# Expert layers in fp32 on TensorE: a third split block product in the first layer, a new order of its passes, and sums on GpSimd

## Chip, cores and metric

The kernel runs on one core of one Trainium2 chip. The metric is the device time of one execution in microseconds (us). Three runs of the kernel before took 2548.86, 2551.64 and 2551.95 us, median 2551.64. Differences below about 0.2% can't be told from none.

## What is computed

`x` is 4096 tokens of 512 values, `ctx` 3202 rows of 512. A gated cross attention comes first, then a gated mixture of experts; both add onto `x`. Only the second half matters here:

```
gates = softmax(layernorm(x) @ w_router + b_router)        # 8 experts
topv, topi = top_k(gates, 2)                               # 2 experts a token
buf[e, slot] = the tokens of expert e                      # 640 slots an expert
h   = gelu(buf[e] @ w1[e] + b1[e])                         # 512 -> 2048
out = h @ w2[e] + b2[e]                                    # 2048 -> 512
y   = gate-weighted sum of a token's two rows of out
x   = x + tanh(g_ffn) * y
```

All of it is in fp32, and the kernel does the experts' matrix products by block schemes with seven products instead of eight (Strassen's, in the form of Winograd): sums of blocks are formed on VectorE ahead, and the products' results are added onto each other in PSUM.

## The kernel before

The attention half, the router and the scatter of the tokens into slots fill the first 1590 us of the trace, and the change doesn't touch them. Then comes a loop over the eight experts (L2428), some 120 us each, in which TensorE's instructions stand in an order written out by hand. So do those of VectorE, ScalarE (ACT) and the load queue: the helpers `dv`, `ac`, `ld` and `mm` (L2019 to L2029) chain every instruction behind the one before it on its engine. GpSimd's gathers and stores are not chained.

**The first layer.** The tokens of an expert lie transposed in `bT` (640 columns, two halves of 320, `HC`), the weights in two halves of four feature blocks. An outer split into seven products, numbered 0 to 6, gives four results per feature block: `lo` and `hi`, each for both halves of the columns. `hidden(e, idx)` (L2257) is one pass, and there are eight, for idx 0 to 7. `product(ps, k)` (L2274) is one of the seven: two matmuls of 320 columns. It may accumulate onto a region that ACT has first filled with another region's content (`nc.scalar.copy(Y, X)`, L2302; `copy(Z, Y)`, L2311). A pass takes six PSUM banks: X in bank 0, Q in 1, Y in 2 or 3 in turn, Z in 4, W in 5. Product 0 goes into X, 4 onto a copy of X in Y, 5 onto a copy of Y in Z, 3 into Q, 1 onto X. VectorE then adds Q (copied to SBUF as `p5`, L2306) onto Y and Z (L2319, L2329) into `hT`, and ACT applies the gelu. Gelus that can't go at once are put into the list `owed`, and `due(n)` (L2282) lets ACT do some of them later.

**The split parts.** For the first six feature blocks, three pairs, products 2 and 6 are not done like that. Each is itself split into seven for a pair of feature blocks: seven matmuls of 160 columns. `parts` (L2217) makes them in three steps, which are laid between the products of another pass: one part in each of the passes 1 to 6 (product 6 of a pair in an odd pass, product 2 in the even pass behind it). A part takes a tile of the transposes' pool `ps_tr` (regions X, W, Q) and a bank for its regions Y and Z. Its steps need sums of weight blocks (`deep_w`, L2204: four VectorE instructions of 128 columns) and of token blocks (`deep_x`, L2193: four of 160 columns, once per expert). At the end four VectorE adds (L2247 to L2250) put its results onto `hT`, and two gelus are owed.

**The order of a pass** is product 0, step one, product 3, step two, product 4, step three, product 1, product 5 (L2297 to L2320), with the ACT copies between. In expert 0 the first four feature blocks have products 0 and 1 done ahead (`early`), and their passes go another way (L2286).

**Around the passes**, the main loop lays further VectorE work: sums of weights for this expert's second half (`w1_sums`), sums for the second layer (`left`, `right`), the bias (L2474, L2476). The second layer is a sequence of plain products and five `deep` groups (R7, R6, R5, R4, R3 in the order of the code; L2396), whose left and right sums are kept in two sets of seven tiles, `sets[0]` and `sets[1]`. `sets[0]` is last read by R4, `u2` by the adds of L2571. The rows that an expert has summed up are stored by five indirect DMAs on GpSimd's queue (`send`, L2510); the next expert's five gathers (L2438) wait until those have landed, and the bias adds wait for the gathers.

Of the kernel before, what the change touches and what calls it, by code (L numbers as in the profile page):

```python
# [8 lines left out]
AF = mybir.ActivationFunctionType  # L9
# [5 lines left out]
P = 128  # L15
# [5 lines left out]
def gated_layer(ctx, tc, x, x_t, ctxt, ctxt_t, ctxt_c, ctxt_r, g_xattn, g_ffn, w_sim, w_sim_r, b_sim, W_qv, W_qv_t, b_qv, b_qv_c, w_router, b_router, w1, b1, w2, b2, out):  # L21
# [1976 lines left out]
    with ExitStack() as s3:  # L1998
# [176 lines left out]
        def rows_of(ti, s):  # L2175
# [9 lines left out]
            k: (b, [flat_set[i][:, q * HH : (q + 1) * HH] for q in range(3)] + [p7[:, i - 5, :HH]])  # L2185
            for k, i, b in (("2", 5, xT[2]), ("6", 6, B22))
        }

        def w_of(k, pair):
            n = 3 * (2 * (pair % 2) + (k == "6"))  # L2190
            return [flat_set[2 + (n + q) // 4][:, (n + q) % 4 * P : ((n + q) % 4 + 1) * P] for q in range(3)]

        def deep_x(k):  # L2193

            b, (t1, t2, t4, t3) = x_of[k]
            b11, b12, b21, b22 = (b[:, c, d : d + HH] for c in range(2) for d in (0, HH))
            return [
                lambda: tt(t1, b12, b11, ALU.subtract),
                lambda: tt(t2, b22, t1, ALU.subtract),
                lambda: tt(t3, b22, b12, ALU.subtract),  # L2200
                lambda: tt(t4, b21, t2, ALU.subtract),
            ]

        def deep_w(e, k, pair):  # L2204
# [12 lines left out]
        def parts(e, k, pair, c_bank):  # L2217

            XWQ = ps_tr.tile([P, DC, P], F32, name=f"d{e}_{k}{pair}", tag="tr").rearrange("p c t -> p (c t)")
            X, W, Q = (XWQ[:, i * HH : (i + 1) * HH] for i in range(3))  # L2220
            YZ = banks[c_bank][:, : 2 * HH]
            Y, Z = YZ[:, :HH], YZ[:, HH:]
            a = w1_forms(e, pair // 2)[int(k)]
            f = pair % 2 * 2 * P
            a11, a12, s3, a22 = (a[:, c, f + r : f + r + P] for r in (0, P) for c in range(2))
            s1, s2, s4 = w_of(k, pair)
            b, (t1, t2, t4, t3) = x_of[k]
            b11, _, b21, b22 = (b[:, c, d : d + HH] for c in range(2) for d in (0, HH))
            dst = hT[:, 0, 2 * pair : 2 * pair + 2, HC:] if k == "6" else hT[:, 1, 2 * pair : 2 * pair + 2, :HC]

            def first():
                mm(X, a11, b11, True, True)
                mm(Q, s1, t1, False, True)
                mm(W, a22, t4, False, True)
                ac(lambda: nc.scalar.copy(Y, X))  # L2235

            def second():
                mm(Y, s2, t2, False, True)
                ac(lambda: nc.scalar.copy(Z, Y))
                mm(X, a12, b21, False, True)  # L2240

            def third():
                mm(Z, s3, t3, False, True)
                mm(Y, s4, b22, False, True)

            adds = [
                lambda: tt(dst[:, :, HH:], dst[:, :, HH:], Q.unsqueeze(1).to_broadcast([P, 2, HH]), ALU.add),  # L2247
                lambda: tt(dst[:, :, :HH], dst[:, :, :HH], XWQ[:, : 2 * HH].rearrange("p (f t) -> p f t", f=2), ALU.add),
                lambda: tt(dst[:, 0, HH:], dst[:, 0, HH:], Y, ALU.add),
                lambda: tt(  # L2250
                    dst[:, 1, :].rearrange("p (d t) -> p d t", d=2), dst[:, 1, :].rearrange("p (d t) -> p d t", d=2),
                    Z.unsqueeze(1).to_broadcast([P, 2, HH]), ALU.add,
                ),
            ]
            return first, second, third, adds, dst

        def hidden(e, idx):  # L2257

            h, f = divmod(idx, KQ)
            col = e * NF + h * KH + f  # L2260
            lo, hi = hT[:, 0, idx, :], hT[:, 1, idx, :]
            bias_of = lambda i, n: (lambda c: b1_t[:, c : c + 1])(e * NF + i // KQ * KH + i % KQ + n * KQ)
            b_lo, b_hi = bias_of(idx, 0), bias_of(idx, 1)
            A = [[a[:, k, f * P : (f + 1) * P] for k in range(2)] for a in w1_forms(e, h)]
            X, Q, Y, Z, W = (banks[i][:, :HC] for i in (0, 1, 2 + idx % 2, 4, 5))
            p5 = p5s[idx % 2]
            there = e == 0 and f in early and h == 0
            split = idx < DEEP_IDX
            part = None
            if 1 <= idx <= DEEP_IDX:  # L2270
                k, pair = ("6", idx // 2) if idx % 2 else ("2", idx // 2 - 1)
                part = parts(e, k, pair, 5 if split else 2 + (idx + 1) % 2)

            def product(ps, k, start=False):  # L2274
                for i in range(2):
                    mm(ps, A[k][i], XS[{2: 6, 6: 2}.get(k, k)][i], start and i == 0, i == 1)

            def step(i):
                if part:
                    part[i]()  # L2280

            def due(n):  # L2282
                ac(*owed[:n])
                del owed[:n]

            if there and idx:  # L2286
                ac(lambda: nc.scalar.copy(Y, early.pop(f)))  # L2287
                step(0)
                product(Y, 4)
                due(1)  # L2290
                ac(lambda: nc.scalar.copy(Z, Y))
                step(1)
                product(Q, 3, True)
                ac(lambda: nc.scalar.copy(p5, Q))
                step(2)
                due(1)
            else:  # L2297
                if there:
                    ac(lambda: nc.scalar.copy(Y, early.pop(f)))
                else:  # L2300
                    product(X, 0, True)
                    ac(lambda: nc.scalar.copy(Y, X))  # L2302
# [8 lines left out]
                ac(lambda: nc.scalar.copy(Z, Y))  # L2311
                step(2)
                due(1)
            if not there:
                product(X, 1)
                ac(lambda: nc.scalar.activation(lo[:, :HC], X, AF.Gelu, bias=b_lo))
            due(len(owed))
            if split:
                dv(lambda: tt(lo[:, HC:], Y, p5, ALU.add))  # L2319
            product(Z, 5)  # L2320
            if part:
                dv(*part[3])
                n = int(k == "2")
                for i in range(2):
                    owed.append(
                        lambda d=part[4][:, i, :], b=bias_of(2 * pair + i, n): nc.scalar.activation(d, d, AF.Gelu, bias=b)
                    )
            ac(lambda: nc.scalar.copy(hi[:, :HC] if split else W, Z))
# [99 lines left out]
        for e in range(E):  # L2428
# [4 lines left out]
            ld(lambda: nc.sync.dma_start(b2_t, b2[e].partition_broadcast(P)))  # L2433
            if e == 0:
                dv(*deep_w(0, "6", 0), *deep_x("6"), *coefs(0))
            cf, ti = cf_of[e], ti_of[e]
            for s in range(NST):
                gather = nc.gpsimd.indirect_dma_start(  # L2438
                    out=accs[s][:, :], out_offset=None,
                    in_=out[:, :], in_offset=rows_of(ti, s), bounds_check=N - 1, oob_is_err=False,  # L2440
                )
# [14 lines left out]
            for idx in range(2 * KQ):  # L2456
# [8 lines left out]
                    dv(*deep_w(e, "2", 0), *deep_x("2"))  # L2465
                if idx in (1, 3):
                    dv(*deep_w(e, "6", 1 + idx // 2), *deep_w(e, "2", 1 + idx // 2))
                if idx in (4, 6, 7):
                    k = (0, 2, 4)[(4, 6, 7).index(idx)]
                    dv(left(1, k, k + 2), left(3, k, k + 2))  # L2470
# [175 lines left out]
```

## Time and profile before

| what | value |
|---|---|
| median of three runs | 2551.64 us |
| profiled execution: its own time | 2551.32 us |
| its span, first to last instruction | 2549.5 us |
| granted TensorE clock, mean | 0.999 |
| TensorE matmul busy | 2533.4 us, 14258 instructions |
| VectorE busy | 1976.1 us |
| ACT busy | 715.4 us |
| GpSimd busy | 274.5 us |

A matmul in fp32 is two weight loads and two MATMULs in the trace. In a group's name, `bank` is one of the six PSUM banks, `d` a part's tile, `l` a tile of the two sets. A bracket behind an instruction says how long its engine had been idle before it, and whose end released it. Rows of the view in order of time merge instructions of one kind that follow each other (x4).

### The profile page before, as it was taken

The numbers are of one execution on the slowest core, as the hardware profiler recorded it, in microseconds if no ns is written. First come the engines' busy times: TensorE is split into PE (matmuls) and PEld (weight loads), VectorE is DVE, ScalarE is ACT, GpSimd is POOL, SyncE is SP. The second block draws the span as 40 slices with busy tenths as digits, with TensorE's granted clock in tenths as the row PEclk, the third lists the DMA queues.
The fourth block names the chain that finished last, engine by engine and source line by source line (L and its number), as shares of the span: only waits on it lengthen the run. The fifth ranks groups of instructions, "written<-read, shape, count | busy, mean of one in ns | idle before, by whom it ended". The sixth has DMA issues, their size and how long they took to land.

```text
span 2549.5 us, 37835 instructions
## 1 busy us (share of the span) xinstructions
PE 2533.4 (99%) x14258; PEld 2215.2 (87%) x14258; DVE 1976.1 (78%) x4118; ACT 715.4 (28%) x1556; POOL 274.5 (11%) x399
## 2 busy tenths in 40 slices
PE   9999999999999999999999999999999999999998
PEld 7788888998988988989989887798888888888978
DVE  8887865876967868859658667887888888787877
ACT  1112302323223123123231144424232332424150
POOL 0101120001001000000000065010101010101010
PEclk9999999999999999999999999999999999999999
DMA  7568795885966957758748895322313141414130
GB/s 259 200 215 292 268 351 177 279 267 167 314 228 204 308 195 239 265 191 284 250 155 291 270 359 182 135 100 95 133 67 133 71 155 44 162 42 158 47 103 21
DMA packets 198407, 489.08 MB, mean 192 GB/s; under 512 B 22462, under 2 KB 79102, under 8 KB 196176
## 3 DMA queue, kind: packets, MB, share of 16 engines
q1 hardware_dynamic: 151984, 386.37, 45.0%
q0 software_dynamic: 21696, 59.07, 6.5%
q10 hardware_dynamic: 24544, 41.21, 4.4%
q8 instruction: 113, 1.85, 0.3%
q14 instruction: 70, 0.57, 0.1%
HBM read 397.40 MB, written 97.52 MB: 194 GB/s over the span
## 4 chain that ended last, share of the span: by engine, by line
PE 88%; issue 5%; DVE 4%; DMA 1%; POOL 1%; another core or an unknown queue 0%; ACT 0%; POOLq 0%; SPq 0%; DVEq 0%; ACTq 0%
PE bank L2029 30%; PE bank L761 21%; PE bank L984 13%; PE bank L1153 6%; PE bank L1510 5%; PE bank L1254 2%; PE d L2029 2%; PE x1p L1755 1%; PE p7d L1510 1%; PE p4d L1510 1%; PE bank L813 1%; PE v L1254 1%; POOL buf_d L1904 1%; PE bps L2105 1%; DVE SM L1023 1%
## 5 line engine op out<-in xcount | busy, mean ns | idle before, releaser
L761 PE MATMUL bank<-Qp,kt 128*128 128x256 f32 x1344 | 305.2, 379 | 0.0
L761 PEld LDWEIGHTS bank<-Qp,kt 128*128 128x128 f32 x1344 | 254.4, 190 | 34.1
L2029 PE MATMUL bank<-w,hT 128*128 128x256 f32 (+1 forms) x1280 | 260.7, 359 | 0.7 <-ACT u L2521 0.7
L2029 PEld LDWEIGHTS bank<-w,hT 128*128 128x128 f32 x1280 | 223.8, 190 | 27.4 <-ACT u L2521 1.1
L761 PE MATMUL bank<-q,kt 128*128 128x256 f32 x1008 | 231.3, 379 | 0.0
L761 PEld LDWEIGHTS bank<-q,kt 128*128 128x128 f32 x1008 | 191.5, 190 | 26.0
L2029 PE MATMUL bank<-bT,w 128*128 128x320 f32 x736 | 211.1, 432 | 0.6 <-ACT bank L2311 0.6
L984 PE MATMUL bank<-dt,vf 128*128 128x128 f32 x1680 | 204.8, 275 | 0.0
L984 PEld LDWEIGHTS bank<-dt,vf 128*128 128x128 f32 x1680 | 196.0, 192 | 0.0
L2029 PEld LDWEIGHTS bank<-bT,w 128*128 128x128 f32 x736 | 136.6, 190 | 50.5 <-ACT bank L2311 1.1
L2029 PE MATMUL bank<-XT,w1s 128*128 128x320 f32 x512 | 156.5, 433 | 0.1
L804 DVE TENSOR_TENSOR M<-M,E_all 128x1024 f32<-128x1024 f32 x80 | 97.9, 1224 | 46.9 <-ACT E_all L721 45.5
L2510 POOL DMA_INDIRECT out<-acc,ti x40 | 39.6, 991 | 802.8 <-DVE acc L2450 796.1
L1755 PE MATMUL x1p<-W,q2T 128*128 128x264 f32 x512 | 117.8, 391 | 1.6 <-PE cnt L1973 0.8
L717 DVE TENSOR_TENSOR E_all<-bank,p5s 128x512 f32<-128x512 f32 x42 | 29.0, 689 | 114.7 <-ACT bank L716 114.6
L1755 PEld LDWEIGHTS x1p<-W,q2T 128*128 128x128 f32 x512 | 97.7, 192 | 19.6 <-issue 1.2
L2029 PEld LDWEIGHTS bank<-XT,w1s 128*128 128x128 f32 x512 | 91.9, 190 | 26.2 <-ACT bank L2287 0.5
L891 DVE TENSOR_TENSOR E_all<-E_all,mb 128x1024 f32<-128x1024 f32 x84 | 101.6, 1216 | 10.3 <-ACT mb L866 10.3
L984 PE MATMUL bank<-E_all,vf 128*128 128x128 f32 x828 | 106.5, 275 | 0.0
L892 ACT ACTIVATE E_all<-E_all 128x1024 f32<-128x1024 f32 x84 | 88.8, 1058 | 49.8 <-DVE E_all L891 49.2
L984 PEld LDWEIGHTS bank<-E_all,vf 128*128 128x128 f32 x828 | 99.8, 192 | 0.3
L2029 PEld LDWEIGHTS bank<-l,l 128*128 128x128 f32 x736 | 92.8, 192 | 8.1 <-ACT bank L2235 0.7
(644 smaller groups left out, 4963.2 us busy)
## 6 DMA issues: line engine op xcount, KB each, us to landing
vf<-vf_d SPq DMA_DIRECT2D x122, 768.0 KB
kt<-kt_d SPq DMA_DIRECT2D x84, 512.0 KB
w<-in_w SPq DMA_DIRECT2D x16, 2048.0 KB
w<-in_w SPq DMA_DIRECT2D x32, 1024.0 KB
kt<-in_ctxt_t SPq DMA_DIRECT2D x84, 384.0 KB
wp<-wt_d SPq DMA_DIRECT2D x56, 520.0 KB
buf_d<-zero SPq DMA_DIRECT2D x80, 129.0 KB
xb<-buf_d SPq DMA_DIRECT2D x39, 258.0 KB
```

What stands on the lines that cost most here:

```text
L717: tt(dst(1, 1), Z, p5, ALU.add)
L761: nc.tensor.matmul(ps[:, jl, :], kts[j][:, KSLOT[p], k, :], B[p][:, k, :], start=start and jl == 0 and k == 0, stop=stop and k == 1, skip_ ...
L804: tt(M, M, e[:, :, h], ALU.max)
L891: live[g]["last"] = tt(e, e, m, ALU.subtract)
L892: live[g]["exp"] = nc.scalar.activation(e, e, AF.Exp)
L984: nc.tensor.matmul(ps, a[:, j, :], rhs[r][:, j, :], start=start and j == 0, stop=j == NP - 1 and (rest is None or add is None), skip_group ...
L1153: nc.tensor.matmul(ps[b], vt[:, j - i * JH, b * P : (b + 1) * P], right(j) if j < NJ else right_c, start=start and j == 0 and b == 0, stop ...
L1254: mm = nc.tensor.matmul(acc[k][:, b, :], a[:, b * P : (b + 1) * P], r, start=start and b == 0, stop=stop, skip_group_check=True,)
L1510: nc.tensor.matmul(ps[m], A[p][:, k, m * P : (m + 1) * P], wt[:, k, :], start=start and k == 0, stop=stop and k == DC - 1, skip_group_chec ...
L1755: mm = nc.tensor.matmul(ps[:, j, :B1], qTs[g][:, c, q * P : (q + 1) * P], W1[:, c, j, :], start=(c == 0), stop=(c == DC - 1))
L2029: return chained("pe", lambda: nc.tensor.matmul(ps, a, b, start=start, stop=stop, skip_group_check=True))
L2510: sc = nc.gpsimd.indirect_dma_start(out=out[:, :], out_offset=rows_of(ti, s), in_=accs[s][:, :], in_offset=None, bounds_check=N - 1, oob_i ...
```

## The change

Product 1 of the three pairs is split as well, under the name "1". It is the third part of a pair; it runs in the odd passes beside part 6, whose steps follow its own, matmul for matmul of a step. Expert 0 splits it for its third pair alone (`first_split`), the others for all three. For the passes with idx below 6 (from 4 on in expert 0):

- The two matmuls of product 1 are left out. `lo` gets a plain copy of X in place of the gelu of X, and the part's four adds and two owed gelus follow at the end of the odd pass, behind those of part 6.
- The order is product 0, step one, product 4, step two, product 3, step three, product 5. Pass 0 has no part.
- Part 1's regions Y and Z are in the bank of the Y of the even passes (2).
- Its sums run on GpSimd: four of token blocks per expert and four of weight blocks per pair, into tiles of `sets[0]` and `u2`. GpSimd's gathers are chained behind them; the stores are not.

```diff
+        flat_low = [t.rearrange("p a b -> p (a b)") for t in sets[0]]
+        x_of["1"] = (B21, [flat_low[6][:, q * HH : (q + 1) * HH] for q in range(3)] + [u2[:, 0, :HH]])
+
+        def first_split(e, idx):
+            return (KQ if e == 0 else 0) <= idx < DEEP_IDX
 
         def w_of(k, pair):
+            if k == "1":
+                return [flat_low[4 + pair % 2][:, q * P : (q + 1) * P] for q in range(3)]
...
-            dst = hT[:, 0, 2 * pair : 2 * pair + 2, HC:] if k == "6" else hT[:, 1, 2 * pair : 2 * pair + 2, :HC]
+            dst = hT[:, int(k == "2"), 2 * pair : 2 * pair + 2, slice(HC, CAP) if k == "6" else slice(0, HC)]
...
+            single = first_split(e, idx)
+            works = [part] if part else []
+            if single and idx % 2:
+                works.insert(0, parts(e, "1", idx // 2, 2 + (idx + 1) % 2))
...
             def step(i):
-                if part:
-                    part[i]()
+                for w in works:
+                    w[i]()
...
+            elif single:
+                product(X, 0, True)
+                ac(lambda: nc.scalar.copy(Y, X))
+                step(0)
+                ac(lambda: nc.scalar.copy(lo[:, :HC], X))
+                due(1)
+                product(Y, 4)
+                ac(lambda: nc.scalar.copy(Z, Y))
+                step(1)
+                product(Q, 3, True)
+                ac(lambda: nc.scalar.copy(p5, Q))
+                due(1)
+                step(2)
...
-            if not there:
+            if not there and not single:
                 product(X, 1)
                 ac(lambda: nc.scalar.activation(lo[:, :HC], X, AF.Gelu, bias=b_lo))
-            due(len(owed))
+            due(1 if single and idx % 2 == 0 else len(owed))
...
             product(Z, 5)
-            if part:
-                dv(*part[3])
+            for w in reversed(works):
+                dv(*w[3])
...
+            def first_w(pair):
+                return chained("gp", *deep_w(e, "1", pair, nc.gpsimd.tensor_tensor))
+
+            chained("gp", *deep_x("1", nc.gpsimd.tensor_tensor))
+            if first_split(e, 0):
+                first_w(0)
             cf, ti = cf_of[e], ti_of[e]
             for s in range(NST):
-                gather = nc.gpsimd.indirect_dma_start(
+                gather = chained("gp", lambda: nc.gpsimd.indirect_dma_start(
...
+                if idx in (1, 3) and first_split(e, idx + 2):
+                    first_w(1 + idx // 2)
```

More of the change, by code (lines that the diff above doesn't have):

```diff
@@ L2187, in gated_layer, with deep_x @@
         }
+        flat_low = [t.rearrange("p a b -> p (a b)") for t in sets[0]]
+        x_of["1"] = (B21, [flat_low[6][:, q * HH : (q + 1) * HH] for q in range(3)] + [u2[:, 0, :HH]])
+        def first_split(e, idx):
+            return (KQ if e == 0 else 0) <= idx < DEEP_IDX
         def w_of(k, pair):
+            if k == "1":
+                return [flat_low[4 + pair % 2][:, q * P : (q + 1) * P] for q in range(3)]
             n = 3 * (2 * (pair % 2) + (k == "6"))
             return [flat_set[2 + (n + q) // 4][:, (n + q) % 4 * P : ((n + q) % 4 + 1) * P] for q in range(3)]
-        def deep_x(k):
+        def deep_x(k, tt=tt):
             b, (t1, t2, t4, t3) = x_of[k]
@@ L2202, in deep_x, with deep_w @@
             ]
-        def deep_w(e, k, pair):
+        def deep_w(e, k, pair, tt=tt):
             a = w1_forms(e, pair // 2)[int(k)]
@@ L2325, in hidden @@
                     owed.append(
-                        lambda d=part[4][:, i, :], b=bias_of(2 * pair + i, n): nc.scalar.activation(d, d, AF.Gelu, bias=b)
+                        lambda d=w[4][:, i, :], b=bias_of(2 * pair + i, n): nc.scalar.activation(d, d, AF.Gelu, bias=b)
                     )
@@ L2435, in gated_layer @@
                 dv(*deep_w(0, "6", 0), *deep_x("6"), *coefs(0))
+            def first_w(pair):
[3 more added lines that the diff above has]
+                first_w(0)
             cf, ti = cf_of[e], ti_of[e]
             for s in range(NST):
-                gather = nc.gpsimd.indirect_dma_start(
+                gather = chained("gp", lambda: nc.gpsimd.indirect_dma_start(
                     out=accs[s][:, :], out_offset=None,
                     in_=out[:, :], in_offset=rows_of(ti, s), bounds_check=N - 1, oob_is_err=False,
-                )
+                ))
                 for i in stored:
```

## Prediction

> **What bounds the kernel now.** I read the page first: how busy each engine is, and the chain of work that ended last.
>
> ```profile
> PE 2533.4 (99%) x14258; PEld 2215.2 (87%) x14258; DVE 1976.1 (78%) x4118; ACT 715.4 (28%) x1556; POOL 274.5 (11%) x399
> PE 88%; issue 5%; DVE 4%; DMA 1%; POOL 1%; another core or an unknown queue 0%; ACT 0%; POOLq 0%; SPq 0%; DVEq 0%; ACTq 0%
> ```
>
> TensorE is busy for all of the span but 16 us, at a granted clock of 0.999. So the kernel ends sooner if TensorE streams fewer columns, and later by every hole that opens between two matmuls. Then I cut one expert (the fourth, first product at 1824.80 us) into its eight passes, with the busy time of each engine.
>
> ```profile
> 1824.80:1830.20 5.40, 5.40 (x23) 3.82 (x22) 5.03 (x17) 1.77 (x4) 1.88 (x2) 1.00 0.79 235
> 1837.50:1844.75 7.25, 7.25 (x35) 5.67 (x34) 5.68 (x19) 3.97 (x10) 3.50 (x4) 1.00 1.05 396
> 1866.60:1876.04 9.44, 9.44 (x43) 7.22 (x42) 6.55 (x13) 4.59 (x12) 0.00 (x0) 1.00 0.00 0
> ```
>
> These are passes 0, 2 and 6: us, then PE, PEld, DVE, ACT, POOL busy, clock, DMA share, GB/s. PE fills every pass; in the view of waits only three matmul waits are left in the whole expert stage (1.5 us). The holes are closed because each PSUM copy on ACT runs behind other products. Last I read the instructions in order of time, for the prices.
>
> ```profile
> 1846.10 0.43 PE L2029 MATMUL d<-l,l 128*128 128x160 f32 x2
> 1846.37 0.43 PE L2029 MATMUL d<-l,w1s 128*128 128x160 f32 x2
> 1846.64 1.24 PE L2029 MATMUL bank<-XT,w1s 128*128 128x320 f32 x4
> 1847.72 0.43 PE L2029 MATMUL bank<-l,l 128*128 128x160 f32 x2
> ```
>
> One matmul of the program is two MATMULs of the trace. From start to start, a 160-column one takes 0.271 us and a product (two of 320 columns) 1.077 us. Cost goes with columns, also at 160.
>
> **What is removed and added on TensorE.** A pair of feature blocks loses product 1 twice: 2 x 1.077 = 2.154 us. It gains seven matmuls of 160 columns: 7 x 0.271 = 1.897. That is -0.257 us a pair. There are 22 pairs (one in expert 0, three in each of the other seven), and the built program agrees: 88 fewer of 320 columns, 154 more of 160. Sum **-5.65 us**, the whole gain.
>
> **The order of a pass.** What I call step one, two and three are the matmuls of a split part that are laid between products. Before: product 0, step one, product 3, step two, product 4, step three, product 1, product 5. In the new passes: product 0, step one, product 4, step two, product 3, step three, product 5. So product 4, which accumulates onto ACT's copy of product 0, now has only step one ahead of it. What such a copy costs uncovered stands in expert 0, where it happens once already:
>
> ```profile
> 1593.22 0.41 ACT L2311 COPY bank<-bank 128x320 f32<-128x320 f32 x1 [0.84 <-PE bank L2029]
> 1593.68 1.34 PE L2029 MATMUL bank<-bT,w 128*128 128x320 f32 x4 [0.55 <-ACT bank L2311]
> 1594.86 0.43 PE L2029 MATMUL d<-bT,w1s 128*128 128x160 f32 x2
> ```
>
> ACT starts 0.20 us after the product's slot ends (so at every L2302), copies for 0.41, and PE starts 0.05 later; the product then takes 1.18 instead of 1.077, since its first weights weren't loaded ahead. Together 0.66 + 0.10 = 0.76 us.
>
> *Pass 0* has no part, so nothing at all stands between product 0 and product 4. In experts 1 to 7 the hole is 0.76 us: **+5.3 us**. (Expert 0 starts splitting at pass 4.)
>
> *Passes 2 and 4* have one part: step one covers 0.81 us, which alone would hide 0.66. But their copy of product 0 goes into the bank (2) which held the new part's two regions in the odd pass before, and ACT waits there until VectorE's last add of that part has read it. I lay out the odd pass from its start: product 0 to 1.08, six matmuls of step one to 2.70, product 4 to 3.78, step two (four) to 4.86, product 3 to 5.94, step three to 7.02, product 5 to 8.10. The copy of product 3 ends at 5.94 + 0.20 + 0.42 = 6.56. From it VectorE adds, as it does now:
>
> ```profile
> 1849.98 0.49 DVE L2319 TENSOR_TENSOR hT<-bank,l 128x320 f32<-128x320 f32 x1 [1.48 <-ACT bank L2311]
> 1850.58 0.49 DVE L2247 TENSOR_TENSOR hT<-hT,d 128x320 f32<-128x320 f32 x1
> 1850.98 0.48 DVE L2248 TENSOR_TENSOR hT<-hT,d 128x320 f32<-128x320 f32 x1
> 1851.38 0.32 DVE L2249 TENSOR_TENSOR hT<-hT,bank 128x160 f32<-128x160 f32 x1
> 1851.61 0.48 DVE L2250 TENSOR_TENSOR hT<-hT,bank 128x320 f32<-128x320 f32 x1
> ```
>
> One add, then four for part 6; now four more for part 1 follow. The first four begin 0.60 after L2319 and the second four at 2.03 (L2250's start and 0.40); four last 1.51. The last ends 3.54 us after 6.60, at 10.14, which is 2.04 into the next pass. There the copy can start at 2.08 instead of 1.28, ends at 2.49, and PE goes on at 2.54; without it PE would be there at 1.08 + 0.81 = 1.89. Hole 0.65 + 0.10 = 0.75 us, in two passes of seven experts: **+10.5 us**. VectorE's earlier work doesn't add to it: the sums queued after pass 2 (1.4 and 1.2 us) end some 4 us into pass 3, ahead of 6.60. Behind the waiting copy ACT holds a part's copy, a copy of product 0 and a gelu, and the copy after product 4, all done before PE needs them (product 4 ends 0.75 later too). Pass 6 has the same wait, but keeps the old order: product 3 and step two cover it.
>
> *Pass 6* has two more gelus owed, those of the new part, in ACT's queue ahead of the copy that product 2 accumulates onto:
>
> ```profile
> 1873.02 0.53 ACT L2316 ACTIVATE hT<-bank,b_t 128x320 f32<-128x320 f32 x1 [0.74 <-PE bank L2029]
> 1873.44 0.55 ACT L2326 ACTIVATE hT<-hT,b_t 128x320 f32<-128x320 f32 x1
> 1874.09 0.41 ACT L2328 COPY bank<-bank 128x320 f32<-128x320 f32 x1
> 1874.97 1.24 PE L2029 MATMUL bank<-XT,w 128*128 128x320 f32 x4
> ```
>
> Now one gelu follows that of product 1, then three: at 1873.44, 1873.87 and 1874.30, and the copy can start 0.55 after the last, at 1874.85. It ends at 1875.26, PE goes on at 1875.31 instead of 1874.97. Hole 0.34 + 0.10 = 0.44 us in all eight experts: **+3.5 us**.
>
> The other new work costs nothing by itself: 88 adds on VectorE (5.3 us more per expert, against 20.8 us idle of 120.1), and 88 copies on ACT (39.2 us busy of 120.1); its gelus stay as many.
>
> **GpSimd.** Each expert gets four sums of 160 columns and four of 128 for each split pair: 120 instructions. No row has such a sum. The nearest are a two-input one of 4 columns (L446, 0.20 us), a select of 128 (0.29), a memset of 512 (0.55) and a power of 4 columns (L444, 1.05). I bound one by 0.20 and 1.05 and take 0.45, near the select and the memset. Six of them now stand ahead of the row stores L2510 (1818.92 before): they start when product 7 of the last-but-one second-layer group frees their tile, about 1816.5, and end at 1819.2, or 1822.8 at the upper bound. Even then the last store goes 1 us late, the gathers of L2438 likewise. Who waits: pair 1's sums are queued behind the five gathers (end 1842.0), are there by 1842.5 (1844.2 at worst), and PE wants them in pass 3, about 1846. Pair 0's last two, queued behind the stores, are there by 1829, wanted at 1836. So no matmul waits for GpSimd: 0.
>
> Beside VectorE, no row shows a GpSimd sum, so its effect there is open. Least: 0. Most I can place: VectorE's adds of 1817.25 free the bank for the last group, 0.34 us before PE uses it at 1818.48; held for one sum of 0.45 to 1.05 us, PE loses 0.2 to 0.8 us with the restart, seven times: 1.5 to 5.7 us. I take 0 and keep 6 for the range. The Trainium skill (GPSIMD Engine Reference, 8. Key points) says that GpSimd shares its SBUF interfaces with VectorE and contends with instructions that have two SBUF inputs. It speaks against this change: by it the sum would rise by up to those 5.7 us, by the rows alone by none. No row here shows it either way.
>
> **Sum.** -5.65 + 5.3 + 10.5 + 3.5 = +13.7 us on the profiled execution, whose own time is 2551.32 us (span 2549.5, 1.8 around it); the median of the runs, 2551.64, is 0.3 above. I predict 2565 us.
>
> **Rivals.**
> 1. *VectorE is done in time.* If its eight adds follow closer, or the copy is released by an earlier add, passes 2 and 4 have no hole: 2554.5 us, +0.1%. For it: step one alone covers the plain copy. Against: adds at a fixed 0.40 spacing in every pass. Chance 0.12; half-sized holes (2560) another 0.06.
> 2. *Faster: the holes close.* Place: product 4 behind ACT's copy. It decides at 0.77 us of holes per expert, the gain of three pairs; pass 0 alone has 0.76. Only with none left does the gain show: 2546 us. For it: today's passes hide every copy. Against: in pass 0 nothing is left to hide it. Chance 0.03.
> 3. *GpSimd slows VectorE* in the tight places, the odd passes' ends too: 2568 to 2576. Chance 0.15.
> 4. *GpSimd is late*: sums of 2 us or more, in which pair 1's would miss pass 3 by some 4 us, seven times: about 2593. Nearest row against it: 0.20. Chance 0.04.
> 5. *It doesn't do what it says*: excluded by the instruction counts above.
>
> **How the numbers follow.** The forecast, 2561 to 2569, has 0.60. Below 0.2% (5.1 us, about what a measurement here can tell from none) lie rival 1's first case, 0.12, and above on the other side rival 2, 0.03; the rest is slower, 0.85. The range 2555 to 2577 takes in the forecast, the half-sized holes, rival 3 and about half of rival 1, and leaves out some 0.13.
>
> **What would show it.** PE holes by ACT's copy (L2302's successor) of 0.7 us in pass 0, in passes 2 and 4 behind L2250's successor, 0.4 us in pass 6 before product 2; odd passes 8.1 us long, pass 0 5.1. Wrong if passes 2 and 4 last 6.2 us, if PE waits for POOL, or if VectorE's sums lengthen beside GpSimd's.

## The result, and the profile after

The changed kernel takes **2565.57 us** (median of six runs, 2564.16 to 2567.77), the kernel before on the same chip 2551.47. The ratio is 1.0057, 95% interval 1.0046 to 1.0068: slower by 0.6%. The forecast was 2565.

First the page of after: busy time of each engine, and the shares of the chain that ended last.

```profile
PE 2536.8 (99%) x14390; PEld 2223.9 (87%) x14390; DVE 2017.5 (79%) x4206; ACT 733.7 (29%) x1644; POOL 343.6 (13%) x519
PE 86%; DVE 5%; issue 5%; DMA 1%; ACT 1%; POOL 1%; another core or an unknown queue 0%; POOLq 0%; SPq 0%; DVEq 0%; ACTq 0%
```

This page nearly hides what happened. TensorE still reads 99%, its busy time has even grown by 3.4 us though it streams fewer columns, and the 16 us that it leaves of the span have become 29. What tells more is the order of time. Two measures follow from it, and they are used for every kernel below:

- **The expert stage**: from the first matmul group `bank<-XT,w1s` to the end of the last matmul. Before 953.15 us, after 967.63: +14.48. (The profiled execution of after took 2567.77 us, 16.45 above that of before; the other 1.97 lie ahead of the experts, in code that the change doesn't touch. The kernel before takes 2544.48 to 2552.95 us on the chips used here; the stage begins at 1584 to 1585 us on the fastest of them and at 1590 to 1593 on the others, so most of that difference lies ahead of it. So the stage can be compared over chips where the whole time can't.)
- **The period of an expert**: from its first product to the next expert's. Before it is 120.03 to 120.06 us in six experts, after 122.14 to 122.15: +2.09 to +2.11 each.

Cutting the same expert of after (the third of the eight, first product at 1828.62) into passes gives passes 0, 1, 2 and 6; the columns are those shown for the kernel before.

```profile
1828.62:1833.69 5.07, 4.57 (x18) 2.96 (x17) 4.70 (x15) 1.59 (x4) 2.85 (x4) 1.00 0.72 224
1833.69:1841.80 8.11, 8.11 (x45) 6.84 (x44) 5.09 (x17) 3.50 (x10) 2.06 (x2) 1.00 1.03 395
1841.80:1848.80 7.00, 6.48 (x31) 4.97 (x30) 6.90 (x19) 3.77 (x10) 5.95 (x9) 1.00 1.04 400
1872.08:1881.92 9.84, 9.70 (x43) 7.09 (x42) 8.22 (x19) 5.40 (x14) 0.00 (x0) 1.00 0.00 0
```

Pass 1 is full (8.11 of 8.11), as each odd pass is. Passes 0 and 2 have about half a microsecond with no matmul, which no pass had before, and pass 6 has 9.70 of 9.84. The view of waits over the expert stage (total, times, longest) says for what TensorE stands still:

```profile
PE bank L2029 <- ACT bank L2311: 9.1, 17, 0.6
PE bank L2029 <- issue: 2.1, 4, 0.5
```

That is 21 waits, three in each of seven experts: product 4 of passes 0, 2 and 4, waiting for ACT's copy of product 0 (L2311 of after). "issue" in the second row is the same place; the view found no releaser there. The view counts less than is lost: a matmul's record reaches 0.16 us beyond its slot, so a hole is the waiting shown, plus 0.16, plus 0.10 for the slow restart. Here is pass 2, where the slots of product 0 and step one end at 1843.69 (VectorE, ACT and TensorE, in order of time):

```profile
1843.35 0.48 DVE L2257 TENSOR_TENSOR hT<-hT,bank 128x320 f32<-128x320 f32 x1
1843.92 0.41 ACT L2311 COPY bank<-bank 128x320 f32<-128x320 f32 x1 [1.49 <-DVE hT L2257]
1844.38 1.34 PE L2029 MATMUL bank<-XT,w1s 128*128 128x320 f32 x4 [0.52 <-ACT bank L2311]
```

The chain stands in the brackets: TensorE is released by ACT's copy, and that copy by VectorE's last add (L2257) of the new part, after ACT had been idle for 1.49 us. From 1843.69 to 1844.38 are 0.69 us, and 0.10 more for the restart (1.34 us for a row of four that takes 1.24 elsewhere).

### The profile page after: what moved, and what is told of

It reads as the page before. It is cut to its first block, busy times and chain, and to the rows that moved or that the text cites. A ratio compares the mean times of both kernels' runs of the same rounds, so it can differ in the third digit from the quotient of the medians.

```text
span 2566.0 us, 38566 instructions
## 1 busy us (share of the span) xinstructions
PE 2536.8 (99%) x14390; PEld 2223.9 (87%) x14390; DVE 2017.5 (79%) x4206; ACT 733.7 (29%) x1644; POOL 343.6 (13%) x519
## 4 chain that ended last, share of the span: by engine, by line
PE 86%; DVE 5%; issue 5%; DMA 1%; ACT 1%; POOL 1%; another core or an unknown queue 0%; POOLq 0%; SPq 0%; DVEq 0%; ACTq 0%
PE bank L2029 28%; PE bank L761 21%; PE bank L984 13%; PE bank L1153 6%; PE bank L1510 5%; PE d L2029 2%; PE bank L1254 2%; PE x1p L1755 1%; PE p7d L1510 1%; PE p4d L1510 1%; PE bank L813 1%; PE v L1254 1%; DMA buf_d<-xn,sidx 1%; PE bps L2105 1%; DVE SM L1023 1%
## 5 line engine op out<-in xcount | busy, mean ns | idle before, releaser
L2029 PE MATMUL bank<-bT,w 128*128 128x320 f32 x560 | 163.8, 433 | 0.6 <-ACT bank L2336 0.6
L2029 PEld LDWEIGHTS bank<-bT,w 128*128 128x128 f32 x560 | 103.2, 190 | 36.5 <-ACT bank L2336 1.1
L2029 PE MATMUL bank<-l,l 128*128 128x128 f32 (+1 forms) x780 | 108.4, 279 | 0.0
L2029 PEld LDWEIGHTS bank<-l,l 128*128 128x128 f32 x780 | 99.7, 192 | 8.0 <-ACT bank L2242 1.6
```

The source lines that it names most:

```text
L2029: return chained("pe", lambda: nc.tensor.matmul(ps, a, b, start=start, stop=stop, skip_group_check=True))
```

## Experiments

The theory is the prediction's: the columns bring -5.65 us, and three uncovered copies on ACT cost more. The rival theory: VectorE, lengthened by GpSimd beside it, is what costs. Each kernel is named by its label. By the columns alone the period would be 120.04 - 3 x 0.257 = 119.27 us.

| kernel | time, us (kernel before, same chip) | ratio, 95% interval | expert stage | period, median |
|---|---|---|---|---|
| before | 2551.47 | 1 | 953.15 | 120.04 |
| after | 2565.57 (2551.47) | 1.0057 [1.0046, 1.0068] | 967.63 | 122.15 |
| e1_hold_p5 | 2560.47 (2550.96) | 1.0038 [1.0025, 1.0052] | 962.45 | 121.39 |
| e2_adds_first | 2557.85 (2550.96) | 1.0030 [1.0019, 1.0042] | 960.15 | 121.10 |
| e3_spread_gelu | 2562.49 (2550.96) | 1.0049 [1.0036, 1.0063] | 964.43 | 121.74 |
| e4_all | 2547.79 (2550.96) | 0.9991 [0.9982, 1.0000] | 949.83 | 119.71 |
| e5_sums_early | 2546.12 (2544.48) | 1.0007 [0.9998, 1.0016] | 953.97 | 120.16 |
| e6_vector_sums | 2549.96 (2544.48) | 1.0021 [1.0012, 1.0030] | 957.50 | 120.61 |
| e7_old_order | 2554.42 (2544.48) | 1.0039 [1.0024, 1.0055] | 962.09 | 121.37 |
| e8_pass0_order | 2559.94 (2544.48) | 1.0058 [1.0043, 1.0073] | 967.66 | 122.15 |
| e9_pair1_vector | 2550.71 (2552.95) | 0.9992 [0.9983, 1.0001] | 953.47 | 119.97 |
| e10_idle_sums | 2556.62 (2552.95) | 1.0013 [1.0004, 1.0022] | 959.40 | 120.85 |
| e11_all_again | 2548.58 (2552.95) | 0.9983 [0.9974, 0.9992] | 949.40 | 119.62 |

### One hole at a time

**e1_hold_p5** covers pass 0: product 3 comes ahead of product 4, and product 5, with what follows it, is held until product 0 of pass 1 has been issued.

```diff
+                if held:
+                    held.pop()()
                 step(0)
...
+                if idx == 0:
+                    product(Q, 3, True)
+                    ac(lambda: nc.scalar.copy(p5, Q))
                 product(Y, 4)
...
+            def ending():            # product 5, its copy, its add, its gelu
...
+            if single and idx == 0:
+                held.append(ending)
+                return
```

> Only pass 0 of the changed kernel differs: product 3 goes ahead of product 4 again, and product 5 is held back until product 0 of pass 1 has been issued, so that both PSUM copies of pass 0 run behind other products. Nothing is removed. Theory of the order (holes come from copies with too little TensorE work in front of the product that needs them): the hole of 0.76 us in pass 0 goes in seven experts, passes 2, 4 and 6 keep theirs: 2565.6 - 5.3 = 2560.3 us. Rival theory (the time went to GpSimd's sums working beside VectorE, and the holes are only where the delay shows): the sums stay as they are, so the delay moves to the next wait and less than 2 us comes back: 2564 us or more.

It took 2560.47 us, and the period falls by 0.76, the hole to the hundredth. In the trace the products of pass 0 follow each other with no bracket, and the row of 8 that holds product 4 lasts 2.32, not 2.42:

```profile
1826.09 1.24 PE L2029 MATMUL bank<-bT,w 128*128 128x320 f32 x4
1827.17 2.32 PE L2029 MATMUL bank<-XT,w1s 128*128 128x320 f32 x8
1829.32 2.32 PE L2029 MATMUL bank<-bT,w 128*128 128x320 f32 x8
```

**e2_adds_first** is for passes 2 and 4: the new part is the first of an odd pass, so that VectorE reads its bank before it adds part 6.

```diff
+            one = parts(e, "1", idx // 2, 2 + (idx + 1) % 2) if single and idx % 2 else None
-            works = [part] if part else []
-            if single and idx % 2:
-                works.insert(0, parts(e, "1", idx // 2, 2 + (idx + 1) % 2))
+            works = [w for w in (one, part) if w]
...
-            for w in reversed(works):
+            for w in works:
```

> Only the order of the two parts of an odd pass differs: part 1 takes its tile first, and its four VectorE adds go ahead of those of part 6, not behind them. The same instructions otherwise. Theory of the order: the copy at the head of passes 2 and 4 then waits for an add that ends 1.4 us earlier, about 0.6 us into the pass, before product 0 has ended; the holes in passes 2 and 4 go (0.79 and 0.85 us in the trace of the changed kernel), those of pass 0 and pass 6 stay: 2565.6 - 11.5 = 2554.1 us. Rival theory (ACT's longer queue, not the read of the bank, makes the copy late): the queue is as long as it was, the holes stay, 2565 us. Second rival (part 6's adds, now last, hold the second bank and its tile): new holes in step two of passes 2 and 4 of some 0.3 us, 2558 us.

It took 2557.85 us. The holes of passes 2 and 4 are gone, which excludes the first rival (ACT's longer queue), but the stage falls by 7.5 us instead of 11.5. A new hole stands in pass 3: part 6 now takes its tile of the transposes' pool second, and its first matmul waits for VectorE's add of part 2 (L2255), which has to read that tile first. The time is that of the expectation's second rival (2558), but the place isn't: that one named step two of passes 2 and 4, behind the adds of part 6, and no hole stands there. Why the adds of part 2 are late stands in the rows ahead of the wait (GpSimd and VectorE in pass 2):

```profile
1842.44 0.53 POOL L2219 TENSOR_TENSOR l<-l,w 128x128 f32<-128x128 f32 x1
1842.57 0.54 DVE L2218 TENSOR_TENSOR l<-w1s 128x128 f32<-128x128 f32 x1
...
1845.30 0.28 DVE L2221 TENSOR_TENSOR l<-w,l 128x128 f32<-128x128 f32 x1
...
1846.91 0.51 PE L2029 MATMUL d<-bT,w1s 128*128 128x160 f32 x2 [0.22 <-DVE hT L2255]
```

The same kind of sum takes 0.54 us beside a sum of GpSimd and 0.28 without one. This gave the rival theory its first support.

**e3_spread_gelu** is for pass 6: one more owed gelu goes behind step two and one more behind step three.

```diff
-                if not part:
+                if not part or idx == DEEP_IDX:
                     due(1)
...
-                due(1)
+                due(2 if idx == DEEP_IDX else 1)
```

> Only pass 6 differs: one more owed gelu goes behind step two and one more behind step three, so that one instead of three stands between product 1's gelu and the copy that product 2 needs. The same instructions otherwise. Theory of the order: the hole of 0.40 us before product 2 of pass 6 goes in eight experts: 2565.6 - 3.2 = 2562.4 us. Rival (ACT has no room in pass 6 at all): the hole moves to product 5 of the same pass, 2565.6 us.

It took 2562.49 us, and the period falls by 0.41. In after three gelus stand ahead of the copy, in e3_spread_gelu one. First pass 6 of after, ACT and TensorE:

```profile
1878.91 1.46 ACT L2351 ACTIVATE hT<-hT,b_t 128x320 f32<-128x320 f32 x3
1879.36 1.24 PE L2029 MATMUL bank<-bT,w1s 128*128 128x320 f32 x4
1880.27 0.42 ACT L2353 COPY bank<-bank 128x320 f32<-128x320 f32 x1
1880.74 1.34 PE L2029 MATMUL bank<-XT,w 128*128 128x320 f32 x4
```

Then the same place in e3_spread_gelu:

```profile
1875.40 0.55 ACT L2351 ACTIVATE hT<-hT,b_t 128x320 f32<-128x320 f32 x1
1875.85 1.24 PE L2029 MATMUL bank<-bT,w1s 128*128 128x320 f32 x4
1876.05 0.41 ACT L2353 COPY bank<-bank 128x320 f32<-128x320 f32 x1
1876.93 1.24 PE L2029 MATMUL bank<-XT,w 128*128 128x320 f32 x4
```

From product 1's start to product 2's are 1.38 us in after and 1.08, a product's own slot, here.

**e4_all** has all three edits.

> The edits of the three runs before together: pass 0 with its product 5 held back, part 1's adds first, pass 6's gelus spread. Theory of the order: no hole is left, and what stays is the gain of the products, 22 pairs of 0.257 us: 2551.5 - 5.7 = 2545.8 us, faster than the kernel before by 0.22%. Rival theory (GpSimd's sums or the added adds cost by themselves): what they cost stays, 2550 us or more.

It took 2547.79 us, 2 us more than expected. The stage falls by 17.8 us, more than by the three edits alone (5.2, 7.5 and 3.2), and the waits of pass 3 that e2_adds_first opened are fewer here. The change that cost 0.57% now gains some 0.1%. **e11_all_again** is the same kernel on a third chip:

> The kernel of e4_all once more, on the chip of e9_pair1_vector and e10_idle_sums, to have the three side by side: an expert stage of 949.5 to 950.2 us, 0.1% below the kernel before; e9_pair1_vector 1 to 2 us below it if the contention theory holds, at it or above by the rival.

There it is at 0.9983, with the interval below 1. So the split itself gains a little, 0.1 to 0.2%, at the edge of what these runs can tell; the uncovered copies made it a loss. In both runs one expert has a period of 119.34 us, 0.07 above what the columns alone would give; the others reach up to 119.96, and TensorE's waits there are those of pass 3 that e2_adds_first showed, but for one of 0.2 us in pass 1 of the seventh expert. Of pass 3 the view of e4_all lists two (total, times, longest); shorter ones are below what it lists:

```profile
PE d L2029 <- DVE hT L2255: 0.6, 2, 0.4
```

### What the order is worth

**e7_old_order** gives the split passes of after the order of before (0, 3, 4, 5 with the steps between):

```diff
                 due(1)
-                product(Y, 4)
-                ac(lambda: nc.scalar.copy(Z, Y))
-                step(1)
                 product(Q, 3, True)
                 ac(lambda: nc.scalar.copy(p5, Q))
+                step(1)
                 due(1)
+                product(Y, 4)
+                ac(lambda: nc.scalar.copy(Z, Y))
                 step(2)
```

> The changed kernel, with its split passes in the order of the kernel before: product 0, step one, product 3, step two, product 4, step three, product 5. Theory of uncovered copies: in pass 0 the hole of 0.76 us only moves, from ahead of product 4 to ahead of product 5 (nothing stands between these two): +5.3 us. In passes 2 and 4 the copy of product 0 has product 3 and step two as cover and its hole closes, while that of product 4 has step three alone, 0.54 us against 0.66: a hole of 0.12 + 0.10 = 0.22 us in two passes of seven experts, +3.1. Pass 6 keeps 0.40: +3.2. With -5.65 by columns and this chip's 2551.0 for the kernel before: 2557. Rival (the order isn't what costs; VectorE's eight adds at a pass's end are): 2562 or more.

It is 9.9 us above the kernel before, not 6: better than the changed kernel by about 4, and about 4 worse than expected. By the number alone the rival (11 or more) is nearer, so the places have to decide. The holes are as expected: pass 0 waits at product 5, and in pass 2 product 5 starts 0.12 us after step three's slots and restarts slowly.

```profile
1837.59 0.43 PE L2029 MATMUL bank<-XT,l 128*128 128x160 f32 x2
1837.98 2.42 PE L2029 MATMUL bank<-bT,w 128*128 128x320 f32 x8
...
1841.39 0.51 PE L2029 MATMUL d<-bT,w1s 128*128 128x160 f32 x2 [0.17 <-DVE hT L2255]
```

The last row is what the expectation lacked: with TensorE sooner, the wait of pass 3 for VectorE appears here too (five times; 0.41 us here with the restart). It makes up some 2 us of the 3 by which the stage (+8.9) is longer than worked out (+5.9); that much of the rival, VectorE late at a pass's end, is true. Beside the best expert of e4_all, this one should have 119.34 + 0.76 + 2 x 0.22 + 0.40 + 0.41 = 121.35 us, and has 121.36.

**e8_pass0_order** uses the old order in pass 0 alone, with nothing held:

```diff
                 step(0)
...
+                if not idx:
+                    product(Q, 3, True)
+                    ac(lambda: nc.scalar.copy(p5, Q))
                 product(Y, 4)
...
+                if idx:
...
```

> The changed kernel, with the old order in pass 0 alone (product 0, 3, 4, 5), and nothing held over as in e1_hold_p5. Theory: without product 1 and without a part there are two copies to hide and only one product to lay over either; product 3 now hides the copy of product 0, and that of product 4 lies open ahead of product 5, 0.76 us again. So the time stays that of the changed kernel, 2565 to 2566. Rival (one product of cover is enough, the copy ahead of product 5 is hidden otherwise): 2560.3.

The period stays at 122.15 us and the stage at 967.66 (after: 967.63). The hole has only moved, ahead of product 5:

```profile
1822.39 2.32 PE L2029 MATMUL bank<-XT,w1s 128*128 128x320 f32 x8
1825.21 1.07 PE L2029 MATMUL bank<-bT,w 128*128 128x320 f32 x3 [0.50 <-ACT bank L2319]
```

Two copies need two covers, and pass 0, without a part and without product 1, has one.

### GpSimd beside VectorE

**e5_sums_early** is e4_all with GpSimd's sums for pair 1 ahead of its gathers, so that they run two passes sooner.

```diff
-            for s in range(NST):
-                gather = ...
+            def gathers(): ...
+            if not e:
+                gathers()
...
                 dv(*deep_w(e, "6", 0), *deep_x("6"), *w1_sums(e, 0, 2))
+                first_w(1)
+                gathers()
...
-                if idx in (1, 3) and first_split(e, idx + 2):
+                if idx in (1, 3) and first_split(e, idx + 2) and not (e and idx == 1):
```

> The kernel of e4_all, but in experts 1 to 7 GpSimd's weight sums of pair 1 go ahead of its gathers, so they run during pass 1 instead of the head of pass 2. Contention theory: what is left in e4_all over the counted columns (2547.8 measured against 2545.3 by columns from this chip's 2551.0) is mostly VectorE late in pass 2 and after, because its sums of two SBUF inputs stretch from 0.28 to 0.43 to 0.54 us beside GpSimd's. In pass 1 VectorE has slack, so the waits of pass 3's step one for L2255 go and the time is 2545.8 to 2546.8. Rival (the rest is lost elsewhere, for instance at the end of the second layer, or the gathers now start some 2 us later and cost as much as is won): 2547.5 to 2549.

It did worse than its rival: 2546.12 us is 1.6 above the kernel before on that chip, and the expert stage is 4.1 us *longer* than that of e4_all. The wait of pass 3 is gone, but VectorE is now stretched in pass 0, where I had not looked for it (its add L2356 starts 9.25 us after the expert's first product, against 8.35 in e4_all), and the delay goes through this add and a gelu on ACT to a copy that part 1 needs. The rival's reasons, the second layer's end and the gathers, are not what the trace shows:

```profile
1822.09 0.53 POOL L2220 TENSOR_TENSOR w<-w 128x128 f32<-128x128 f32 x1
1822.24 0.57 DVE L2207 TENSOR_TENSOR p<-bT 128x160 f32<-128x160 f32 x1
...
1827.07 0.48 DVE L2356 TENSOR_TENSOR hT<-bank,l 128x320 f32<-128x320 f32 x1
1827.59 0.56 ACT L2357 ACTIVATE hT<-hT,b_t 128x320 f32<-128x320 f32 x1 [1.52 <-DVE hT L2356]
...
1828.41 0.45 ACT L2246 COPY bank<-bank 128x160 f32<-128x160 f32 x2
...
1828.81 0.51 PE L2029 MATMUL bank<-u,w 128*128 128x160 f32 x2 [0.57 <-ACT bank L2246]
```

Each of seven experts has this wait.

**e6_vector_sums** is e4_all with every sum of the new part on VectorE, none on GpSimd.

```diff
-                return chained("gp", *deep_w(e, "1", pair, nc.gpsimd.tensor_tensor))
+                return dv(*deep_w(e, "1", pair))
...
-            chained("gp", *deep_x("1", nc.gpsimd.tensor_tensor))
...
-                dv(*deep_w(e, "6", 0), *deep_x("6"), *w1_sums(e, 0, 2))
+                dv(*deep_w(e, "6", 0), *deep_x("6"))
+                dv(*deep_x("1"))
+                first_w(0)
+                dv(*w1_sums(e, 0, 2))
```

> The kernel of e4_all, but all sums of the third split product (four of token blocks per expert, four of weight blocks per pair) are formed by VectorE; GpSimd forms none. VectorE gets 16 more instructions an expert, some 4.5 us by their rows (0.28 to 0.3 each), and loses the stretching beside GpSimd, which cost it some 1.9 us an expert. Theory (VectorE has 20 us of slack an expert, and GpSimd's help is worth nothing to TensorE): 2545.5 to 2548, as e4_all or a little better, no VectorE instruction of two SBUF inputs longer than in the kernel before. Rival (GpSimd's help is needed, because the sums of the first pair now stand ahead of this expert's other sums between two experts, or those of the other pairs push VectorE's last add past the next pass): 2552 or more, with new waits of TensorE for VectorE.

The rival held in its mechanism: no sum is stretched, pass 3 has no wait, and yet the stage is 7.7 us longer than e4_all's. Its eight further sums (four of token blocks, four for pair 0) delay VectorE in pass 0 as in e5_sums_early, and more:

```profile
1827.92 0.54 PE L2029 MATMUL bank<-l,l 128*128 128x160 f32 x2 [0.15 <-ACT bank L2242]
1831.06 0.54 PE L2029 MATMUL bank<-u,w 128*128 128x160 f32 x2 [0.70 <-ACT bank L2246]
```

So GpSimd's sums slow VectorE, and still, with VectorE's work in this order, the kernel is better with them on GpSimd; other orders weren't run. The two runs leave one question: does a sum on GpSimd delay VectorE by itself, or only the results that someone waits for? **e9_pair1_vector** is e4_all with pair 1's four sums alone on VectorE; **e10_idle_sums** adds, to that, four sums on GpSimd in their place, into a block that pair 0 no longer needs and pair 2 fills anew later, so nobody reads them.

```diff
+                if idx == 1 and first_split(e, 3):
+                    dv(*deep_w(e, "1", 1))
+                    # the next two lines in e10_idle_sums only:
+                    spare = [flat_low[4][:, q * P : (q + 1) * P] for q in range(3)]
+                    chained("gp", *[lambda: nc.gpsimd.tensor_tensor(spare[0], spare[1], spare[2], ALU.add) for _ in range(4)])
-                if idx in (1, 3) and first_split(e, idx + 2):
-                    first_w(1 + idx // 2)
+                if idx == 3 and first_split(e, 5):
+                    first_w(2)
```

> The kernel of e4_all, but the four weight sums of pair 1's third split product are formed by VectorE, in its order behind the sums that follow pass 1; GpSimd keeps the token sums and those of pairs 0 and 2. Contention theory: in e4_all the 2.3 us that the expert stage is above its columns (949.83 us from its first split-layer matmul to the last, against 953.15 - 5.65 = 947.5) are TensorE's waits for VectorE's adds at the end of pass 2, and VectorE is late there because four of GpSimd's sums run beside some six of its own and stretch them from 0.28 to about 0.5 us. Four more sums of 0.28 cost VectorE about 1.1 us, the stretching some 1.5 to 1.8. So the adds come about 0.5 us sooner, the waits of pass 3 for L2255 go, and the expert stage lasts 947.7 to 948.6 us: some 4.5 to 5.5 us (0.2%) below the kernel before. Rival (VectorE has too much to do in pass 2, whoever forms the sums): the waits stay or grow, the expert stage lasts 950 to 953.

> The kernel of e9_pair1_vector, and in the place where GpSimd formed pair 1's sums it adds four blocks of 128 x 128 into a tile that nobody reads. Nothing waits for these four. Contention theory: VectorE's sums of two SBUF inputs stretch beside them as before, with four more in its queue than in e4_all, so its adds at the end of pass 2 come 0.5 to 1.5 us later than in e9_pair1_vector, and TensorE waits for L2255 in pass 3 of most experts: the expert stage is 3 to 8 us longer than that of e9_pair1_vector. Rival (what made VectorE late was its own amount of work or a wait for GpSimd's results): the same as e9_pair1_vector within 1 us.

e9_pair1_vector did not gain: its period is 119.97, 0.35 above e11_all_again on the same chip, and the wait for L2255 comes in six experts (2.3 us). That is what its rival said (waits that stay or grow). But its own four sums take VectorE 0.9 us, and GpSimd's first two sums of pair 2 slid into the place left free and stretched VectorE again; so it doesn't separate the two theories. (Its stage also holds one wait of 1.5 us in expert 0, for ACT's L2300, that e11_all_again hasn't. Its cause stays open; e10_idle_sums has it too, so it drops out of what follows.) e10_idle_sums does separate them: with four sums that nobody waits for, the period grows by 0.88 us, and the time by 5.9. First e9_pair1_vector, then e10_idle_sums, in pass 2 (VectorE, GpSimd) and at the wait of pass 3:

```profile
1845.03 0.28 DVE L2221 TENSOR_TENSOR l<-w,l 128x128 f32<-128x128 f32 x1
1845.23 0.28 DVE L2218 TENSOR_TENSOR l<-w 128x128 f32<-128x128 f32 x1
...
1847.58 0.51 PE L2029 MATMUL d<-bT,w1s 128*128 128x160 f32 x2 [0.38 <-DVE hT L2255]
```

```profile
1844.06 2.42 POOL L2520 TENSOR_TENSOR l<-l 128x128 f32<-128x128 f32 x4
...
1844.89 0.54 DVE L2218 TENSOR_TENSOR l<-w 128x128 f32<-128x128 f32 x1
1845.46 0.50 DVE L2219 TENSOR_TENSOR l<-l,w 128x128 f32<-128x128 f32 x1
...
1849.30 0.51 PE L2029 MATMUL d<-bT,w1s 128*128 128x160 f32 x2 [1.29 <-DVE hT L2255]
```

The sums shown are at 0.28 where GpSimd is idle and at 0.50 to 0.54 beside its four. TensorE's wait grows from 0.38 to 1.29. Adds with an input from PSUM aren't lengthened: in e4_all L2254 takes 0.47 us at 1842.54, beside a sum of GpSimd at 1842.56, and it takes 0.48 in the kernel before.

## Why the prediction was right

The mechanism is the predicted one, and each term was measured, per expert and for all. That the time is met to 0.6 us (2565.57 against 2565) is partly luck: single terms are off by 0.3 to 1.0 us and cancel in part.

| step | predicted, us | measured, us |
|---|---|---|
| columns: 88 matmuls of 320 out, 154 of 160 in | -5.65 (three pairs: -0.77) | -0.70 for an expert's three pairs, in the best experts of e4_all and e11_all_again |
| pass 0, nothing over the copy | 7 x 0.76 = +5.3 | 0.76 each; e1_hold_p5 takes 5.2 from the stage |
| passes 2 and 4, copy behind VectorE's last add | 14 x 0.75 = +10.5 | 0.79 and 0.85: +11.5 |
| pass 6, three gelus ahead of the copy | 8 x 0.44 = +3.5 | 0.40 in the trace, 0.41 by e3_spread_gelu: +3.2 |
| GpSimd | 0 | no hole of the changed kernel is left for it: below |
| sum | +13.7 | +14.48 (expert stage: +14.73 in experts 1 to 7, -0.25 in expert 0) |

For one expert, from the 119.34 us of e4_all's best: 119.34 + 0.76 + 0.79 + 0.85 + 0.40 = 122.14, and the trace has 122.15. The 0.07 us that the columns bring less than worked out were not traced to a place. Expert 0 has its split pair and its hole of pass 6, together some +0.1 us; it gains 0.25 because a wait of the kernel before for a part's copy (0.16 us at 1603.17, some 0.4 as a hole) is gone, which the prediction left out. (The expert that the prediction calls the fourth, first product at 1824.80, is the third; the periods are alike, so nothing hangs on it.)

*Passes 0, 2, 4 and 6* went as laid out, down to the releaser. The term that was sized least well is that of passes 2 and 4: ACT starts its copy 0.08 to 0.09 us after the end of VectorE's last add, not 0.04, and in pass 4 the add ends 0.04 later than laid out, so the holes are 0.79 and 0.85 instead of 0.75. That a copy's bank is freed by VectorE's *last* add was the term worth most, and it could be found ahead only by laying one odd pass out in order: products, steps and VectorE's queue. Step one covers 0.81 us, more than the copy's 0.66; the copy was late for another reason. e2_adds_first shows this: with the adds in the other order the same cover is enough.

*Rival 1* (VectorE done in time, 2554.5) and *rival 2* (the holes close, 2546) are not what the kernel does, but its edits come to them: e2_adds_first is rival 1's case but for the new wait in pass 3, e4_all is rival 2's, and rival 2's point of decision, 0.77 us of holes an expert, is passed there (119.62 to 119.71 against 120.04). *Rival 4* (GpSimd late) is out: no matmul waits for GpSimd in any view of waits. Its sums of 128 columns took 0.49 to 0.52 us in three of four lines (0.45 was assumed, from 0.20 to 1.05). The fourth line, L2220, has 0.81, because it takes 1.37 us in each pair 2, where it runs beside a VectorE sum of 1024 columns (1.22 us).

*GpSimd at 0* is right as a number and **wrong as a reason**. The prediction held the effect on VectorE open, from 0 to 5.7 us, and looked for it in the second layer's end, where it cost nothing (from the start of the last group to the next expert's first product 6.32 us, before and after). It is large elsewhere: in experts 1 to 7 the eight groups of 128-column sums took VectorE 48.2 us before and 58.2 after (their rows added up). In the changed kernel no matmul waits in pass 3 for VectorE's adds, so this fell into time in which nobody waited for it. That the holes which ACT's copies made gave it this time is argued, not shown by itself; for it speaks that when e2_adds_first, e4_all and e7_old_order take holes away, the next wait is VectorE's. The prediction's own mark against itself ("wrong if VectorE's sums lengthen beside GpSimd's") has thus come true without the time being wrong.

The Trainium skill (GPSIMD Engine Reference, 8. Key points) had it: GpSimd shares its SBUF interfaces with VectorE and contends with instructions of two SBUF inputs. The runs agree, in the kind of instruction too: in after, sums of two SBUF tiles go from 0.28 us (128 columns) to as much as 0.58 and from 0.42 (256) to as much as 0.71, while adds with an input from PSUM (320 columns) stay at 0.47 to 0.49. The prediction weighed the rule at one place only.

Rival 3 (GpSimd slows VectorE in the tight places, 2568 to 2576) is right in that VectorE is slowed, and wrong in that TensorE waits for it; its 2576 is more than the 5.7 us that the prediction works out, and no run shows the rest. How little was missing e5_sums_early shows: in the order of e4_all, the same sums two passes sooner cost 4 us.

## What to carry to other kernels

When product columns are taken out of a stage that TensorE fills, ask what those matmuls were covering: here the two matmuls of product 1 (1.077 us) were also the cover over a copy that costs 0.76 us when it lies open, and their removal cost more than it saved until each copy had other work over it. Follow a copy's start, not only its length, through the reads that free its target. And when sums are moved to GpSimd, count their time on VectorE too, wherever VectorE adds two SBUF tiles beside them; beside VectorE's adds from PSUM no lengthening was seen here.

## What the runs showed of the hardware that was not expected

- Four sums on GpSimd (2.42 us) delay VectorE beside them by some 0.86 us, with no data between the two: from the start of VectorE's first 128-column sum of pass 2 (L2218) to its add L2351 it takes 3.61 us in e9_pair1_vector and 4.47 in e10_idle_sums. By the length of a row: 128 columns 0.28 us free and mostly 0.43 or 0.54 beside GpSimd, 160 columns 0.32 and up to 0.74, 256 columns 0.42 and up to 0.71 (the last two in e7_old_order).
- It goes the other way too: in after, GpSimd's 128-column sum L2220 takes 1.37 us in all eight places where it starts beside VectorE's sum of 1024 columns (1.22 us), and 0.47 to 0.50 in 13 of the other 14.
- Left open: why some sums beside GpSimd stay at 0.28 while their neighbours take 0.54, and why a few are lengthened where the trace shows only a gather on GpSimd (0.58 at 1842.55 in e9_pair1_vector). Spans on GpSimd are rough in the trace, and no run takes this apart.
